# Local layers with four tiles in flight: shares divided on GpSimd, averages feature-major, projection of two tiles at once

## The chip, the cores and the metric

The kernel runs on one NeuronCore of a Trainium2 chip. The core has five engines that run side by side, each in its own order: TensorE (PE in the profile, with its weight loads shown as PEld), VectorE (DVE), ScalarE (ACT), GpSimd (POOL) and SyncE (SP), which here only issues transfers. Engines wait for each other through semaphores. Matmuls read SBUF and write PSUM[...]; GpSimd does not read PSUM in this kernel. The metric is the device time of one execution in microseconds.

## The reference, cut to what matters

The whole program is a stack of four layers (cross attention, routed feed-forward, windowed attention and so on). The change touches only the third layer's second half, a local transformer of six blocks (DEPTH = 6) over x of shape (4, 512, 128), with 16 heads of 64 features and windows of 32 tokens:

```python
def local_attention(q, k, v):          # q, k normalised and rotated
    bq = q.reshape(b, h, nw, w, d)     # w = 32
    bk2, bv2 = look(bk), look(bv)      # this window and the one before it: 64 keys
    sim = einsum('bhwie,bhwje->bhwij', bq, bk2) * 8.0
    sim = where(mask, -max, sim)       # only the 32 keys before a query and itself
    attn = softmax(sim, -1)
    out = einsum('bhwij,bhwje->bhwie', attn, bv2)
...
for i in range(DEPTH):
    x = attn_layer(shift_tokens(x), Wqkv[i], q_scale[i], k_scale[i], Wo[i]) + x
    x = ffn_layer(shift_tokens(x), ...) + x
```

`attn_layer` projects x to q, k and v (1024 features each), divides q and k by their length in each head, applies a rotation by position, attends as above and projects the 1024 features back to 128 with Wo. All values are fp32.

## The kernel before

The function `local_transformer` works on 96 tiles of 128 tokens: six blocks, four rows of the batch, four tiles a row (`tt` is 0 to 3). The residual stream Y is kept feature-major: 128 feature partitions by 512 tokens for each row. The loop at the end of the function runs over n, and one turn of it, here called a period, works on several tiles at once: T (tile n) is projected to q, k and v and rotated, T1 (tile n - 1) has its q and k transposed and its scores and softmax computed, T2 (tile n - 2) has its probabilities transposed, its averages taken and projected. Beside them F, a whole row of 512 tokens, goes through one of the four phases of the feed-forward: phase 0 takes the moments and normalises, phase 1 transposes and does the gate products of two chunks, phase 2 the gate of the third chunk and two up products, phase 3 the last up product and the down product. The order of the statements is written by hand (`manual_schedule`), and each engine executes its own instructions in exactly that order.

What a tile goes through, with the lines of the profile:

- `queries_or_keys` (L1780, L1782): a matmul of 512 columns, four a tile (two for q, two for k), and its square on ScalarE.
- `rotate` (L1790, L1793, L1802, L1803): two products and a sum over squares on VectorE, then an addition on GpSimd.
- `normalise` (L1813 to L1822): the inverse lengths, small operations on GpSimd and ScalarE, and four products on GpSimd.
- `turned` (L583 with rc, L1830 or L1832, L1834): q, then k, transposed on TensorE and copied by ScalarE. For k, GpSimd first copies the last 32 keys of the tile before (L1830), or zeros (L1832), to the front of kT.
- `scores` (L1878, L1887): mask and scores, 64 rows by 32 columns of the array at a time, into the two banks "sc".
- `softmax` (L1897, L1898, L1903): largest value and subtraction on VectorE, exponential on ScalarE. The sum is not taken here: v has a 65th column of ones (L1851), so that the averages carry their own sum.
- `probabilities` (L583 with P, L1908): P transposed and copied.
- `average` (L1918): four pairs of heads at a time, stationary P^T (64 keys by 32 queries), moving v (64 keys by 65), output token-major in the two banks "av".
- `normalised` (L1927, L1928): reciprocal of the 65th column and product, on VectorE, to attn.
- `attended` (L583 with attn, L1937): attn transposed to feature-major aT.
- `project_out` and `residual` (L1942, L1949): eight accumulating matmuls over 128 tokens, and the addition to Y in two halves of 64 partitions.
- `values` (L1857, L1858, and the DMAs from L1860 on): v for both halves of the heads, copied to v1, and shifted by a window into v2 by transfers on SP's queue.

The PSUM pair "sc" is shared by the scores and by the feed-forward's products, and the pair "av" by averages and projection. A new use of a pair waits for the last reader of the old one. Two banks "tr" serve all transposes and the values in turn, two banks "mm" the q and k products. P, PT, attn and aT have one buffer each, v1 and v2 three, the rotated tiles six.

## Time and profile before

| | |
|---|---|
| median of the runs | 2501.84 us (2493.18 to 2504.8, 3 runs) |
| profiled execution | 2497.58 us |
| its span, first to last instruction | 2495.8 us |
| granted TensorE clock, mean | 0.951 |
| busy PE / DVE / ACT / POOL | 90% / 70% / 52% / 55% |
| L1780 matmuls, first to last | 533.7 to 2150.7 us |

The span holds everything from the first instruction to the last. In a group's row the first numbers are the total busy time and the mean time of one instruction, and after the bar stands the idle time of its engine just before it and what ended that idle time. [...] how fast matmuls follow each other is read from the timeline, by the difference between the starts of neighbouring rows. An fp32 matmul stands in the trace as two records. A timeline row gives the start, the duration from the first start to the last end, the engine, the line, what is written and read, and how many instructions it merges; in brackets is the idle time before it with its releaser.

### The profile page before, as it was taken

To read this page: it belongs to the slowest core of one execution; us is meant where nothing else is said; L and a number is where in the kernel's file an instruction comes from. 1 tells how busy PE (TensorE), PEld (TensorE's weight loads), DVE (VectorE), ACT (ScalarE), POOL (GpSimd) and SP (SyncE) were. 2 spreads that over 40 slices of the span, in tenths; PEclk is the share of its full clock that TensorE was granted. 3 is DMA by queue.
4 is the path that set the end of the run, shared out by engine and by line. 5 is a ranking of instruction groups with operands and counts; after the bars stand their busy time and mean duration, and the time that the engine had idled before them with its cause. 6 is when DMAs were issued, how large, how long until landed. Compare 5 with 4: busy or idle time off the path is not lost.

```text
span 2495.8 us, 86737 instructions
## 1 busy us (share of the span) xinstructions
PE 2257.5 (90%) x37341; PEld 1487.1 (60%) x37341; DVE 1746.9 (70%) x3818; ACT 1292.4 (52%) x2379; POOL 1383.5 (55%) x1948
## 2 busy tenths in 40 slices
PE   7959879968999999999999999999999999978676
PEld 3537644536666666666666666666666666634365
DVE  5526355757788787778888888788788888655522
ACT  3513225545666556666666666556556666524232
POOL 2241232347667666676667766766667666432433
PEclk9959889989999999999999999999999999979788
DMA  6210110014411121111211121111211111111022
GB/s 162 84 39 23 37 42 2 1 49 95 120 34 35 30 57 50 27 35 35 69 35 35 30 76 35 30 31 39 65 35 35 33 29 35 29 39 47 21 74 83
DMA packets 134297, 116.14 MB, mean 47 GB/s; under 512 B 29505, under 2 KB 102700, under 8 KB 133916
## 3 DMA queue, kind: packets, MB, share of 16 engines
q1 hardware_dynamic: 128373, 102.81, 15.8%
q0 software_dynamic: 4608, 7.35, 0.9%
q8 instruction: 296, 4.85, 0.8%
q14 instruction: 85, 0.70, 0.1%
q10 hardware_dynamic: 935, 0.43, 0.1%
HBM read 42.84 MB, written 21.52 MB: 26 GB/s over the span
## 4 chain that ended last, share of the span: by engine, by line
PE 72%; DVE 15%; issue 4%; ACT 3%; DMA 2%; POOL 2%; another core or an unknown queue 2%; SPq 1%; POOLq 0%; ACTq 0%; DVEq 0%
PE ps_tr L583 12%; PE ps_mm L1780 10%; PE ps_av L1942 6%; PE ps_av L1918 5%; PE ps_tr L1857 5%; PE ps_sc L1887 4%; DVE xn L523 3%; PE ps_sc L1977 3%; PE ps_sc L1988 3%; PE ps_sc L2000 2%; PE ps L774 2%; PE ps L1313 2%; PE ps L783 2%; PE ps L1682 2%
## 5 line engine op out<-in xcount | busy, mean ns | idle before, releaser
L1803 POOL TENSOR_TENSOR rc<-rc,rs 128x512 f32<-128x512 f32 x384 | 489.5, 1276 | 385.4 <-DVE rs L1793 329.5
L1780 PE MATMUL ps_mm<-wqk,y 128*128 128x512 f32 x768 | 396.9, 599 | 10.5 <-DVE rs L1793 7.3
L1822 POOL TENSOR_TENSOR rc<-rc,rn_y 128x512 f32<-128x512 f32 x384 | 388.7, 1044 | 7.5
L1790 DVE TENSOR_TENSOR rc<-ps_mm,tabs 128x512 f32<-128x512 f32 x384 | 262.5, 684 | 137.8 <-ACT sq L1782 123.4
L1782 ACT ACTIVATE sq<-ps_mm 128x512 f32<-128x512 f32 x384 | 231.4, 603 | 166.9 <-PE ps_mm L1780 119.3
L1793 DVE TENSOR_TENSOR rs<-ps_mm,tabs 128x512 f32<-128x512 f32 x384 | 261.5, 681 | 1.6 <-POOL rc L1803 1.4
L1802 DVE TENSOR_REDUCE ss<-sq 128x8 f32<-128x512 f32 x384 | 259.5, 676 | 0.0
L583 PE MATMUL ps_tr<-cst,rc 128*128 128x128 f32 x1536 | 210.7, 280 | 6.8 <-issue 4.1
L1918 PEld LDWEIGHTS ps_av<-v,PT 64*32 64x32 f32 x12288 | 138.1, 105 | 124.5 <-PE ps_tr L583 55.8
L1942 PE MATMUL ps_av<-aT,wo 128*128 128x128 f32 x1536 | 199.6, 283 | 3.4 <-issue 3.2
L1942 PEld LDWEIGHTS ps_av<-aT,wo 128*128 128x128 f32 x1536 | 181.0, 193 | 12.7 <-issue 4.0
L583 PEld LDWEIGHTS ps_tr<-cst,rc 128*128 128x128 f32 x1536 | 164.6, 141 | 26.7 <-issue 4.7
L1918 PE MATMUL ps_av<-v,PT 64*32 64x65 f32 x12288 | 169.9, 225 | 4.6 <-DVE attn L1928 2.1
L1887 PE MATMUL ps_sc<-kT,qT 64*32 64x64 f32 x12288 | 146.8, 224 | 28.9 <-issue 26.8
L1018 POOL DMA_INDIRECT back<-ye,to x80 | 78.0, 975 | 162.0 <-DVE ye L1132 120.4
L1887 PEld LDWEIGHTS ps_sc<-kT,qT 64*32 64x32 f32 x12288 | 140.1, 105 | 39.1 <-issue 31.4
L1780 PEld LDWEIGHTS ps_mm<-wqk,y 128*128 128x128 f32 x768 | 124.6, 192 | 60.7 <-issue 48.8
L764 ACT ACTIVATE P<-ps,deltaT 77x512 f32<-77x512 f32 x192 | 115.4, 682 | 77.5 <-PE ps L758 69.9
L1903 ACT ACTIVATE P<-P 128x1024 f32<-128x1024 f32 x96 | 101.5, 1057 | 92.1 <-DVE P L1898 92.1
L1814 ACT ACTIVATE rn_y<-ss 128x32 f32<-128x32 f32 x96 | 22.0, 229 | 238.4 <-POOL ss L1813 238.4
L1834 ACT COPY qT<-ps_tr 128x512 f32<-128x512 f32 x192 | 103.3, 589 | 74.6 <-PE ps_tr L583 74.3
L1834 ACT COPY kT<-ps_tr 128x512 f32<-128x512 f32 x192 | 103.3, 589 | 66.2 <-PE ps_tr L583 65.9
(394 smaller groups left out, 4439.6 us busy)
## 6 DMA issues: line engine op xcount, KB each, us to landing
v<-v SPq DMA_DIRECT2D x432, 65.0 KB
v<-v SPq DMA_DIRECT2D x96, 195.0 KB
wqk<-in_L_ffn_Wqkv_dram SPq DMA_DIRECT2D x24, 256.0 KB
sent<-xn SPq DMA_DIRECT2D x2, 2210.0 KB
xe<-sent SPq DMA_DIRECT2D x16, 260.0 KB
back<-xn SPq DMA_DIRECT2D x2, 2048.0 KB
raw<-in_L_ffn_W_dram SPq DMA_DIRECT2D x8, 512.0 KB
yb<-back SPq DMA_DIRECT2D x16, 256.0 KB
```

The lines of the kernel that those rows point to most:

```text
L583: PE.transpose(t[:, i], src[:, i], ident)
L1780: PE.matmul(t, lhs, T.w[2 * kind + c], start=True, stop=True)
L1782: SC.activation(sq, t, AF.Square)
L1790: V.tensor_tensor(a, t, bc(T.tabs[:, 2 * kind, tt], [128, 8, LD], 1), ALU.mult)
L1793: V.tensor_tensor(r.rearrange("p h (x d) -> p h x d", x=2), t.rearrange("p h (x d) -> p h x d", x=2)[:, :, ::-1], bc(T.tabs[:, 2 * kind + ...
L1802: V.tensor_reduce(T.ss[:, kind, 8 * c : 8 * c + 8], sq, AX.X, ALU.add)
L1803: G.tensor_tensor(a, a, r, ALU.add)
L1822: G.tensor_tensor(a, a, bc(y[:, o : o + 8], [128, 8, LD], 2), ALU.mult)
L1834: SC.copy(t[:, 4 * c : 4 * c + 4, lead:], to_features(T.rot[kind, c].rearrange("p (k x) d -> p k (x d)", x=2)),)
L1887: PE.matmul(T.banks[32 * w : 32 * w + 32, z, k], T.qT[r, k, 32 * w : 32 * w + 32], T.kT[r, k, 32 * w : 32 * w + 64], start=False, stop=Tru ...
L1918: PE.matmul(T.means[32 * w : 32 * w + 32, x0, k], T.PT[r, 4 * g + k, 32 * w : 32 * w + 32], (T.v1 if w % 2 else T.v2)[r, x0, 4 * g + k], s ...
L1942: PE.matmul(t, T.wo[:, c], T.aT[:, c], start=(c == 0), stop=(c == 7))
```

## The change

The period now holds four tiles. T and T1 do what they did. T2 only sums its exponentials: the new `sums` takes the 16 sums and their reciprocals on VectorE, and the new `shares` multiplies P by them on GpSimd, in place, in two products of 128 by 512. T3 (tile n - 3) has its probabilities transposed, averaged and projected. P has two buffers, and v loses its column of ones.

`average` swaps the operands: v is stationary (64 keys by 64 features) and P^T moves (64 keys by 32 queries), so that the output is feature-major, 64 partitions at a time. The two calls, pairs of heads 0 to 3 and 4 to 7, fill the same pair of banks, with no reader between them. `normalised` is gone, and `attended` is two copies by ScalarE from PSUM into one half of an aT for 256 tokens; its eight transposes are gone. `project_out` and `residual` run for every second tile, over 256 columns.

In the order of statements: both halves of the average stand ahead of the first key product; `sums` and `shares` stand behind the second rotation; `attended` stands ahead of `turned(T1, 1)`, where before it stood behind the third rotation. The feed-forward phases, and the loading of the next block's weights, start one period later, and the loop has one more turn.

```diff
-                    T.v1 = vp.tile([128, 2, LH // 2, LD + 1], F32, name="v1")
-                    T.v2 = vp.tile([128, 2, LH // 2, LD + 1], F32, name="v2")
-                    G.memset(T.v1[:, :, :, LD : LD + 1], 1.0)
+                    T.v1 = vp.tile([128, 2, LH // 2, LD], F32, name="v1")
+                    T.v2 = vp.tile([128, 2, LH // 2, LD], F32, name="v2")
...
+            def sums(T):
+                T.sum = small.tile([128, LH // 2, 2], F32, name="la_sum")
+                V.tensor_reduce(T.sum, T.P, AX.X, ALU.add)
+                V.reciprocal(T.sum, T.sum)
+
+            def shares(T):
+                for g in range(2):
+                    k = slice(4 * g, 4 * g + 4)
+                    P = T.P[:, k].rearrange("p k z d -> p (k z) d")
+                    rec = T.sum[:, k].rearrange("p k z -> p (k z)")
+                    G.tensor_tensor(P, P, bc(rec, [128, 8, LD], 2), ALU.mult)
...
             def average(T, g):
                 if g == 0:
-                    T.attn = tp.tile([128, LH // 2, 2, LD], F32, name="attn", bufs=1)
-                T.means = pair("av")[:, :, : 4 * LD + 4].rearrange("p x (k d) -> p x k d", d=LD + 1)
-                for k in range(4):
+                    T.means = pair("av").rearrange("p s (k q) -> p s k q", q=64)
+                for k in range(4 * g, 4 * g + 4):
                     for w in range(4):
                         for x0 in range(2):
                             r = slice(64 * (x0 ^ (w // 2)), 64 * (x0 ^ (w // 2)) + 64)
+                            q = 32 * (w % 2)
                             PE.matmul(
-                                T.means[32 * w : 32 * w + 32, x0, k],
-                                T.PT[r, 4 * g + k, 32 * w : 32 * w + 32],
-                                (T.v1 if w % 2 else T.v2)[r, x0, 4 * g + k],
-                                start=True, stop=True,
+                                T.means[64 * x0 : 64 * x0 + 64, w // 2, k, q : q + 32],
+                                (T.v1 if w % 2 else T.v2)[r, x0, k],
+                                T.PT[r, k, 32 * w : 32 * w + 32], start=True, stop=True,
                             )
...
             def attended(T):
-                flat = T.attn.rearrange("p k x d -> p k (x d)")
-                T.aT = tp.tile([128, LH // 2, 128], F32, name="aT", bufs=1)
-                for g in range(2):
-                    SC.copy(T.aT[:, 4 * g : 4 * g + 4], to_features(flat[:, 4 * g : 4 * g + 4]))
+                if T.tt % 2 == 0:
+                    T.aT = tp.tile([128, LH // 2, 256], F32, name="aT", bufs=1)
+                else:
+                    T.aT = T.before.aT
+                for s in range(2):
+                    o = 128 * (T.tt % 2) + 64 * s
+                    SC.copy(T.aT[:, :, o : o + 64], T.means[:, s])
...
-                t = pair("av")[:, 0, :128]
+                t = pair("av")[:, 0, :256]
...
-                m, phase = divmod(n - 6, 4)
+                m, phase = divmod(n - 7, 4)
...
-                    if n % 16 == 7 and T.i + 1 < DEPTH:
+                    if n % 16 == 8 and T.i + 1 < DEPTH:
...
-                if T2:
-                    average(T2, 0)
+                if T3:
+                    average(T3, 0)
                 if T1:
                     turned(T1, 0)
+                if T3:
+                    average(T3, 1)
                 if T:
                     queries_or_keys(T, 1, 0)
-                if T2:
-                    normalised(T2, 0)
-                if T:
                     rotate(T, 0, 1)
                 if T2:
-                    average(T2, 1)
+                    sums(T2)
+                    shares(T2)
+                if T3:
+                    attended(T3)
                 if T1:
                     turned(T1, 1)
                 if T:
                     queries_or_keys(T, 1, 1)
-                if T2:
-                    normalised(T2, 1)
-                if T:
                     rotate(T, 1, 0)
-                if T2:
-                    attended(T2)
...
-                if T2:
-                    project_out(T2)
-                    residual(T2)
+                if T3 and T3.tt % 2:
+                    project_out(T3)
+                    residual(T3)
```

More of the change, by code (lines that the diff above doesn't have):

```diff
@@ L1857, in values @@
                 PE.matmul(t, src[:, 128 * tt : 128 * tt + 128], T.wv[:, x0], start=True, stop=True)
-                SC.copy(T.v1[:, x0, :, 0:LD], t)
+                SC.copy(T.v1[:, x0], t)
                 if x0 == 0:
@@ L1893, in softmax @@
             def softmax(T):
-                P = tp.tile([128, LH // 2, 2, LD], F32, name="P", bufs=1)
+                T.P = tp.tile([128, LH // 2, 2, LD], F32, name="P", bufs=2)
+                P = T.P.rearrange("p k z d -> p z k d")
                 mx = small.tile([128, 2, LH // 2], F32, name="la_mx")
                 V.tensor_reduce(mx, T.banks, AX.X, ALU.max)
-                V.tensor_tensor(
-                    P.rearrange("p k z d -> p z k d"), T.banks,
-                    bc(mx, [128, 2, LH // 2, LD], 3), ALU.subtract,
-                )
-                T.P = P.rearrange("p k z d -> p k (z d)")
-                SC.activation(T.P, T.P, AF.Exp, scale=8.0)
+                V.tensor_tensor(P, T.banks, bc(mx, [128, 2, LH // 2, LD], 3), ALU.subtract)
+                SC.activation(T.P, T.P, AF.Exp, scale=8.0)
+            def sums(T):
[8 more added lines that the diff above has]
+                    G.tensor_tensor(P, P, bc(rec, [128, 8, LD], 2), ALU.mult)
             def probabilities(T):
                 T.PT = tp.tile([128, LH // 2, 128], F32, name="PT", bufs=1)
+                P = T.P.rearrange("p k z d -> p k (z d)")
                 for g in range(2):
-                    SC.copy(T.PT[:, 4 * g : 4 * g + 4], to_features(T.P[:, 4 * g : 4 * g + 4]))
+                    SC.copy(T.PT[:, 4 * g : 4 * g + 4], to_features(P[:, 4 * g : 4 * g + 4]))
             def average(T, g):
                 if g == 0:
-                    T.attn = tp.tile([128, LH // 2, 2, LD], F32, name="attn", bufs=1)
-                T.means = pair("av")[:, :, : 4 * LD + 4].rearrange("p x (k d) -> p x k d", d=LD + 1)
-                for k in range(4):
+                    T.means = pair("av").rearrange("p s (k q) -> p s k q", q=64)
+                for k in range(4 * g, 4 * g + 4):
                     for w in range(4):
@@ L1917, in average @@
                             r = slice(64 * (x0 ^ (w // 2)), 64 * (x0 ^ (w // 2)) + 64)
+                            q = 32 * (w % 2)
                             PE.matmul(
-                                T.means[32 * w : 32 * w + 32, x0, k],
-                                T.PT[r, 4 * g + k, 32 * w : 32 * w + 32],
-                                (T.v1 if w % 2 else T.v2)[r, x0, 4 * g + k],
-                                start=True, stop=True,
-                            )
-            def normalised(T, g):
-                den = small.tile([128, 2, 4], F32, name="la_den")
-                V.reciprocal(den, T.means[:, :, :, LD])
-                V.tensor_tensor(
-                    T.attn[:, 4 * g : 4 * g + 4].rearrange("p k x d -> p x k d"),
-                    T.means[:, :, :, 0:LD], bc(den, [128, 2, 4, LD], 3), ALU.mult,
-                )
-            def attended(T):
-                flat = T.attn.rearrange("p k x d -> p k (x d)")
-                T.aT = tp.tile([128, LH // 2, 128], F32, name="aT", bufs=1)
-                for g in range(2):
-                    SC.copy(T.aT[:, 4 * g : 4 * g + 4], to_features(flat[:, 4 * g : 4 * g + 4]))
+                                T.means[64 * x0 : 64 * x0 + 64, w // 2, k, q : q + 32],
+                                (T.v1 if w % 2 else T.v2)[r, x0, k],
+                                T.PT[r, k, 32 * w : 32 * w + 32], start=True, stop=True,
+                            )
+            def attended(T):
+                if T.tt % 2 == 0:
[5 more added lines that the diff above has]
+                    SC.copy(T.aT[:, :, o : o + 64], T.means[:, s])
             def project_out(T):
-                t = pair("av")[:, 0, :128]
+                t = pair("av")[:, 0, :256]
                 for c in range(8):
@@ L1945, in residual @@
             def residual(T):
-                t = T.out
-                for r, o in ((slice(0, 64), 0), (slice(64, 128), 1)):
-                    dst = Y[T.b][r, 128 * T.tt + o : 128 * T.tt + o + 128]
+                t, o0 = T.out, 128 * (T.tt - 1)
+                for r, o in ((slice(0, 64), o0), (slice(64, 128), o0 + 1)):
+                    dst = Y[T.b][r, o : o + 256]
                     V.tensor_tensor(dst, t[r], dst, ALU.add)
@@ L2033, in local_transformer @@
             SC.preload_act_table_set(EXP_LN)
-            for n in range(len(tiles) + 10):
-                T = tiles[n] if n < len(tiles) else None
-                T1 = tiles[n - 1] if 0 <= n - 1 < len(tiles) else None
-                T2 = tiles[n - 2] if 0 <= n - 2 < len(tiles) else None
-                m, phase = divmod(n - 6, 4)
+            for n in range(len(tiles) + 11):
+                T, T1, T2, T3 = (tiles[n - k] if 0 <= n - k < len(tiles) else None for k in range(4))
+                m, phase = divmod(n - 7, 4)
                 F = rows[m] if 0 <= m < len(rows) else None
                 if T:
-                    if n % 16 == 7 and T.i + 1 < DEPTH:
+                    if n % 16 == 8 and T.i + 1 < DEPTH:
                         loaded[T.i + 1] = load(T.i + 1)
@@ L2053, in local_transformer @@
                     queries_or_keys(T, 0, 0)
-                if T2:
-                    probabilities(T2)
+                if T3:
+                    probabilities(T3)
                 if T:
@@ L2060, in local_transformer @@
                     ff_stage(F, phase, False)
-                if T2:
-                    average(T2, 0)
+                if T3:
+                    average(T3, 0)
                 if T1:
                     turned(T1, 0)
+                if T3:
+                    average(T3, 1)
                 if T:
                     queries_or_keys(T, 1, 0)
-                if T2:
-                    normalised(T2, 0)
-                if T:
                     rotate(T, 0, 1)
                 if T2:
-                    average(T2, 1)
+                    sums(T2)
+                    shares(T2)
+                if T3:
+                    attended(T3)
                 if T1:
@@ L2088, in local_transformer @@
                     rotate(T, 1, 1)
-                if T:
                     normalise(T)
@@ L2092, in local_transformer @@
                     softmax(T1)
-                if T2:
-                    project_out(T2)
-                    residual(T2)
+                if T3 and T3.tt % 2:
+                    project_out(T3)
+                    residual(T3)
                 if F and phase == 0:
```

## The prediction

> **What bounds the kernel now.** The table of busy shares comes first, then the chain that ended last, then the costliest groups, then the timeline of single periods, because shares average over stages with different limits.

> ```profile
> PE 2257.5 (90%) x37341; PEld 1487.1 (60%) x37341; DVE 1746.9 (70%) x3818; ACT 1292.4 (52%) x2379; POOL 1383.5 (55%) x1948
> ...
> PE 72%; DVE 15%; issue 4%; ACT 3%; DMA 2%; POOL 2%; another core or an unknown queue 2%; SPq 1%; POOLq 0%; ACTq 0%; DVEq 0%
> ...
> L1803 POOL TENSOR_TENSOR rc<-rc,rs 128x512 f32<-128x512 f32 x384 | 489.5, 1276 | 385.4 <-DVE rs L1793 329.5
> L1822 POOL TENSOR_TENSOR rc<-rc,rn_y 128x512 f32<-128x512 f32 x384 | 388.7, 1044 | 7.5
> L1918 PE MATMUL ps_av<-v,PT 64*32 64x65 f32 x12288 | 169.9, 225 | 4.6 <-DVE attn L1928 2.1
> ```

> TensorE is busy 90% and carries 72% of the chain, so removing its work looks like the way to gain. The changed stage, the local layers, runs from the first L1780 matmul (533.7 us) to the last (2150.7): 1617 us for 96 tiles, 16.84 us each. Its loop has four kinds of period, by the feed-forward phase in each. The windows view of four neighbours (columns: length, busy PE, PEld, DVE, ACT, POOL):

> ```profile
> 1211.30:1228.50 17.20, 16.87 (x331) 11.25 (x330) 11.79 (x20) 12.57 (x22) 11.41 (x17) 1.00 0.32 93
> 1228.50:1246.07 17.57, 17.57 (x333) 11.55 (x332) 14.00 (x23) 8.94 (x17) 12.26 (x18) 1.00 0.09 25
> 1246.07:1260.85 14.78, 14.63 (x330) 10.63 (x329) 14.15 (x30) 7.69 (x16) 9.14 (x14) 1.00 0.16 40
> 1260.85:1277.97 17.12, 16.78 (x333) 11.31 (x332) 15.32 (x25) 11.95 (x23) 12.60 (x19) 1.00 0.13 34
> ```

> They are phases 2, 3, 0, 1, together 66.67 us. In phase 0 VectorE is busy 14.15 of 14.78 us and the critical chain there leaves TensorE for it. So TensorE is the bound, but VectorE, ScalarE and GpSimd, each in order, are close behind in single places. The timelines of TensorE, ScalarE and GpSimd in phase 2 show the place I hold decisive, the start of the scores:

> ```profile
> 1219.25 1.02 PE L1780 MATMUL ps_mm<-wqk,y 128*128 128x512 f32 x2
> 1220.11 1.04 PE L583 MATMUL ps_tr<-cst,attn 128*128 128x128 f32 x8
> 1221.07 0.41 PE L1878 MATMUL ps_sc<-maskw,identb 64*32 64x512 bf16 x8
> 1221.30 1.46 PE L1887 MATMUL ps_sc<-kT,qT 64*32 64x64 f32 x128
> ...
> 1219.01 1.07 ACT L1834 COPY kT<-ps_tr 128x512 f32<-128x512 f32 x2 [0.31 <-PE ps_tr L583]
> 1220.36 0.60 ACT L1782 ACTIVATE sq<-ps_mm 128x512 f32<-128x512 f32 x1 [0.27 <-ACT kT L1834]
> 1220.85 1.07 ACT L1937 COPY aT<-ps_tr 128x512 f32<-128x512 f32 x2
> ...
> 1218.14 1.27 POOL L1803 TENSOR_TENSOR rc<-rc,rs 128x512 f32<-128x512 f32 x1 [1.61 <-DVE rs L1793]
> 1219.36 0.40 POOL L1830 COPY kT<-kT 128x256 f32<-128x256 f32 x1
> 1220.77 1.28 POOL L1803 TENSOR_TENSOR rc<-rc,rs 128x512 f32<-128x512 f32 x1 [1.02 <-PE ps_tr L583]
> ```

> Scores (L1887) need kT from two engines: the two copies on ScalarE (done 1220.08) and the 32-key lead on GpSimd (done 1219.76). Both have over 1.2 us to spare, because TensorE still does a key matmul and the transposes of attn after the transposes of k.

> **The change, part by part** (TensorE costs from start to next start).

> Transposes of attn removed: eight, pitch 0.11, -0.87 us a tile. ScalarE keeps two 0.59 us copies, now from the averages.

> Projection of two tiles: now 16 records in 1.89 us per tile (1272.65 to 1274.54). N=512 records follow each other at 0.43 us, so N=256 ones at 0.216: 3.46 us for two tiles, -0.16 a tile. But every second period has 3.46 and the other none: it falls into phases 1 and 3, already the longer ones.

> Averages: 64 records a half in both versions. Now eight 64x32 array tiles run side by side, 0.64 us plus 0.15 until the next matmul: 0.79. Then four 64x64 ones, 64 weight columns and 32 moving. No row shows 64x64. Low end: the present 0.79. High end: pairs of tiles taken one after the other, 0.107 us a pair of loads, 16 per half, plus 0.15: 1.9. Weight loads last 105 ns at 32 columns and 192 at 128, 0.9 ns a column; [...] I take 1.1 (loads 0.93 plus the gap), nearer the load row: +0.62 a tile for two halves. [...]

> TensorE in sum: -0.87 - 0.16 + 0.62 = -0.41 us a tile.

> VectorE: two reciprocals and two products out (0.8 a half, 1.65), one sum over 1024 elements (as L1897, 1.22) and a reciprocal (0.2) in; residual halves in number. It is near equal, but the sum stands between the second and third rotation.

> GpSimd: two products in, of L1822's form (1.044 each): +2.09 us, minus the 0.13 us memset of ones. [...] The row gives 1.044 against 0.692 for L1928, 1.5 times[...]. I use the row. Busy goes to 13.4 of 16.7 us, no bound by total. Behind these products in its queue stands the kT lead copy, and behind that scores wait.

> ScalarE: the two attended copies move from behind the fourth square to ahead of the kT copies, 1.1 us; the kT copies, the fourth square, the fourth rotation and the softmax are behind them.

> At nothing: v DMAs (2048 for 2080 bytes a row, one period more until use); the weight loads of the next layer, one period later on SP, seven periods (117 us) ahead of their use; with that cover gone, one wait a layer. Pipeline one tile deeper: one more thin period in the drain, +4 us once.

> **The four periods worked out.** Times are from the first query matmul. Phase 3: queries 0.86, transposes of P 0.87, queries 0.86, feed-forward 0.95, average 1.1, turned 0.93, average 1.1, keys at 6.65, turned at 7.5, keys, TensorE ready for scores at 9.3. ScalarE: third square 7.7 to 8.3 (it starts 1.1 after its matmul, as at 1252.03), attended to 9.3, first kT copy to 9.85, second to 10.4, fourth square to 10.95. VectorE: rotations (1.8 each) to 6.2, sum and reciprocal to 7.6. GpSimd: products 7.65 to 9.75, lead copy to 10.15. Scores start at 10.2; now 9.99 (1238.49). So 0.9 us of TensorE saving becomes a wait. Then 1.4 scores, 3.46 projection, 1.72 values, 2.58 feed-forward: 19.4.

> Phase 0: VectorE first has 1.5 us of residual, then the layer-norm moments (1.15) between rotations: sum done at 8.3, products to 10.4, lead 10.85, scores 10.9 (now 9.78). Fourth square 10.65, rotation to 12.5, softmax subtraction to 14.9, exponential 16.0, first v copy 16.6. No projection: TensorE is done at 14.0 but the next transposes of P need the bank of that v copy, so they start at 16.6 (now 16.08).

> Phase 1 from there: normalisation on VectorE to 1.8, rotations to 5.4, sum to 6.85, products to 9.0, lead 9.4, scores 9.45 (now 9.11); then 1.4 + 3.46 + 1.72 + 1.72: 17.75 (now 15.82).

> Phase 2: lead 9.9, scores 9.95 (now 10.0), values to 13.1; the up projection needs the score banks, which the softmax frees at 10.95 + 1.8 + 2.4 = 15.15 (now 14.1); no projection covers this; plus 1.72: 16.9.

> Sum 16.6 + 17.75 + 16.9 + 19.4 = 70.65 against 66.67: +1.0 us a tile, +96 us. With averages at 0.85 instead of 1.1 phases 0 and 2 shorten by half a us each, +70. I take +88, and +4 for the drain: 2497.58 (the profiled execution; its span 2495.8) becomes 2590. The median of the runs, 2501.84, is 4 above that execution: 2594, given as 2592.

> **Rivals.**

> Averages slow: [...] at 1.9 the keys come 1.6 us later each period and TensorE is ready after the lead copy: some +1.5 us a tile in all, 2645. For it: half the array tiles, in pairs. Against: queued loads of other tiles now start 7 ns apart.

> Waits half absorbed: were the lead copy always in time, phases 1 and 3 would lose 1.05 and 0.65 less: +0.57 a tile, 2560; with quick averages as well +0.36, 2540.

> The other side: TensorE alone decides, -0.41 x 96 + 4 = -35: 2467; with averages at 0.79, -99. Place: the first score matmul. It decides if kT, lead included, is there when TensorE is ready (8.2 to 9.3 us) in every period and the softmax leaves the banks before TensorE returns to them. For it: TensorE's 90%; GpSimd has idle time. Against: the sum is queued behind two rotations, and its end at 7.6 plus 2.1 plus 0.4 is 10.1.

> **How the numbers follow.** Chances: waits as worked out 0.57 (own range 2555 to 2625), slow averages 0.16, half absorbed 0.15, TensorE alone 0.12. The range 2505 to 2675 leaves out the last case and the tail of the second. A time 0.5% from before is what a measurement of this kernel can tell from no change. Faster 0.10 and same 0.04 come from the last case and the edge of the third, slower 0.86.

> **What would show it.** Right: GpSimd products before the lead copy at 9.5 to 11 us into each period; TensorE idle before the first score matmul, released by GpSimd's kT copy; the up projection waiting for the softmax in every fourth period; even and odd periods differing by some 2.5 us. Wrong: TensorE busy over 97% between 700 and 2000 us, no wait at the scores, or averages at 0.8 or over 1.5 us a half.

## The result, and the profile after

The changed kernel takes 2606.61 us (median of 4 runs, 2599.62 to 2612.25) against 2498.09 for the kernel before on the same chip: a ratio of 1.0421, 95% interval 1.0396 to 1.0446. The forecast was 2592 in a range of 2505 to 2675. The profiled execution took 2599.62 us with a span of 2597.8, 102 more than before.

The page of the changed kernel, busy shares and chain:

```profile
PE 2258.4 (87%) x35805; PEld 1446.1 (56%) x35805; DVE 1680.5 (65%) x3530; ACT 1279.6 (49%) x2379; POOL 1568.4 (60%) x2044
...
PE 64%; DVE 16%; issue 6%; ACT 4%; POOL 4%; DMA 2%; SPq 1%; another core or an unknown queue 1%; POOLq 0%; ACTq 0%; DVEq 0%
```

TensorE has 1536 records fewer and is busy as long as before; its share of the chain fell from 72% to 64%, and "issue" (nothing visible to wait for) and GpSimd gained. The local stage, from the first L1780 matmul (529.9 us) to the last (2239.0), takes 1709.1 us, 17.80 a tile, against 1617.0 and 16.84: 92 of the 102 us. Four neighbouring periods, phases 1, 2, 3 and 0 (length, busy PE, PEld, DVE, ACT, POOL):

```profile
1307.13:1326.95 19.82, 18.18 (x326) 12.37 (x325) 13.86 (x23) 12.55 (x23) 16.42 (x23) 1.00 0.13 34
1326.95:1344.19 17.24, 15.12 (x308) 9.16 (x307) 11.17 (x16) 12.03 (x22) 12.47 (x18) 1.00 0.07 19
1344.19:1363.64 19.45, 19.20 (x326) 12.63 (x325) 14.17 (x21) 8.96 (x18) 15.07 (x19) 1.00 0.16 44
1363.64:1377.69 14.05, 12.75 (x306) 8.65 (x305) 12.97 (x26) 7.53 (x16) 12.68 (x17) 1.00 0.09 21
```

They sum to 70.56 us. The long periods are the ones with a projection (326 records), and the short ones no longer keep TensorE busy: 12.75 of 14.05. The timelines of VectorE, GpSimd and TensorE in the last of these periods show the place that the prediction held decisive:

```profile
1370.37 1.21 DVE L1902 TENSOR_REDUCE la_sum<-P 128x16 f32<-128x1024 f32 x1
1371.62 0.25 DVE L1903 RECIPROCAL la_sum<-la_sum 128x16 f32<-128x16 f32 x1
...
1372.01 2.04 POOL L1911 TENSOR_TENSOR P<-P,la_sum 128x512 f32<-128x512 f32 x2 [0.64 <-DVE la_sum L1903]
1374.00 0.39 POOL L1830 COPY kT<-kT 128x256 f32<-128x256 f32 x1
...
1371.79 1.02 PE L1780 MATMUL ps_mm<-wqk,y 128*128 128x512 f32 x2
1372.74 0.41 PE L1876 MATMUL ps_sc<-maskw,identb 64*32 64x512 bf16 x8
1374.45 1.49 PE L1885 MATMUL ps_sc<-kT,qT 64*32 64x64 f32 x128 [1.30 <-POOL kT L1830]
```

Sum, reciprocal, two products, lead copy, and only then the scores: TensorE stood idle 1.30 us. In phase 3 the same wait is 0.25 us; in phases 1 and 2 the scores wait 0.21 us for ScalarE's kT copy instead. Two more waits of the same four periods, in phase 1 (transposes of P for the bank of the v copies) and in phase 2 (up projection for the softmax):

```profile
1309.58 1.14 PE L583 MATMUL ps_tr<-cst,P 128*128 128x128 f32 x8 [1.43 <-ACT v L1856]
1342.39 1.96 PE L1995 MATMUL ps_sc<-xnT,lw 128*128 128x512 f32 x4 [1.91 <-DVE P L1897]
```

The table of TensorE's waits over the whole run (us in total, times, longest):

```profile
PE ps_sc L1885 <- POOL kT L1830: 42.0, 52, 3.1
PE ps_tr L583 <- ACT v L1856: 36.9, 25, 2.4
PE ps_sc L1885 <- issue: 30.8, 16, 2.8
PE ps_sc L1995 <- DVE P L1897: 27.7, 19, 1.9
```

The first, second and fourth were forecast: they are the three waits just shown. In the kernel before, the only wait of this stage near that size was "scores, issue", 26.8 us. The third line, idle time without a releaser, was in neither the forecast nor any of its rivals.

### The profile page after: what moved, and what is told of

It is laid out like the page before. It is cut to its first block, busy times and chain, and to the rows that moved or that the text cites. A ratio compares the mean times of both kernels' runs of the same rounds, so it can differ in the third digit from the quotient of the medians.

```text
span 2597.8 us, 83333 instructions
## 1 busy us (share of the span) xinstructions
PE 2258.4 (87%) x35805; PEld 1446.1 (56%) x35805; DVE 1680.5 (65%) x3530; ACT 1279.6 (49%) x2379; POOL 1568.4 (60%) x2044
## 4 chain that ended last, share of the span: by engine, by line
PE 64%; DVE 16%; issue 6%; ACT 4%; POOL 4%; DMA 2%; SPq 1%; another core or an unknown queue 1%; POOLq 0%; ACTq 0%; DVEq 0%
PE ps_mm L1780 10%; PE ps_tr L583 8%; PE ps_av L1949 7%; PE ps_av L1929 5%; PE ps_sc L1885 4%; PE ps_tr L1855 4%; PE ps_sc L1995 3%; PE ps_sc L1984 3%; PE ps_sc L2007 2%; POOL P L1911 2%; DVE P L1897 2%; DVE la_mx L1896 2%; PE ps L774 2%; DVE rc L1790 2%; ACT kT L1834 2%
## 5 line engine op out<-in xcount | busy, mean ns | idle before, releaser
L1803 POOL TENSOR_TENSOR rc<-rc,rs 128x512 f32<-128x512 f32 x384 | 487.8, 1273 | 238.8 <-DVE rs L1793 170.3
L1780 PE MATMUL ps_mm<-wqk,y 128*128 128x512 f32 x768 | 408.4, 615 | 11.0 <-DVE rs L1793 7.7
L1822 POOL TENSOR_TENSOR rc<-rc,rn_y 128x512 f32<-128x512 f32 x384 | 388.2, 1042 | 7.5
L1782 ACT ACTIVATE sq<-ps_mm 128x512 f32<-128x512 f32 x384 | 236.2, 616 | 259.1 <-issue 137.9
L1793 DVE TENSOR_TENSOR rs<-ps_mm,tabs 128x512 f32<-128x512 f32 x384 | 261.1, 680 | 1.5 <-POOL rc L1803 1.4
L1911 POOL TENSOR_TENSOR P<-P,la_sum 128x512 f32<-128x512 f32 x192 | 196.1, 1042 | 74.3 <-DVE la_sum L1903 59.4
L1929 PEld LDWEIGHTS ps_av<-PT,v 64*64 64x64 f32 x12288 | 201.6, 134 | 64.3 <-issue 24.3
L1929 PE MATMUL ps_av<-PT,v 64*64 64x32 f32 x12288 | 222.7, 221 | 0.6 <-issue 0.5
L583 PE MATMUL ps_tr<-cst,rc 128*128 128x128 f32 x1536 | 205.1, 276 | 3.9 <-POOL rc L1822 3.9
L583 PEld LDWEIGHTS ps_tr<-cst,rc 128*128 128x128 f32 x1536 | 172.3, 141 | 60.3 <-issue 39.8
L1885 PEld LDWEIGHTS ps_sc<-kT,qT 64*32 64x32 f32 x12288 | 129.9, 105 | 114.4 <-POOL kT L1830 66.2
L1949 PE MATMUL ps_av<-aT,wo 128*128 128x256 f32 x768 | 183.1, 392 | 2.2 <-ACT aT L1943 1.2
L1780 PEld LDWEIGHTS ps_mm<-wqk,y 128*128 128x128 f32 x768 | 125.3, 193 | 67.7 <-issue 46.4
L1949 PEld LDWEIGHTS ps_av<-aT,wo 128*128 128x128 f32 x768 | 144.8, 194 | 25.8 <-issue 1.8
L1834 ACT COPY qT<-ps_tr 128x512 f32<-128x512 f32 x192 | 103.3, 589 | 92.8 <-PE ps_tr L583 92.4
L1898 ACT ACTIVATE P<-P 128x1024 f32<-128x1024 f32 x96 | 101.5, 1057 | 90.5 <-DVE P L1897 90.5
```

The source lines that it names most:

```text
L583: PE.transpose(t[:, i], src[:, i], ident)
L1780: PE.matmul(t, lhs, T.w[2 * kind + c], start=True, stop=True)
L1782: SC.activation(sq, t, AF.Square)
L1793: V.tensor_tensor(r.rearrange("p h (x d) -> p h x d", x=2), t.rearrange("p h (x d) -> p h x d", x=2)[:, :, ::-1], bc(T.tabs[:, 2 * kind + ...
L1803: G.tensor_tensor(a, a, r, ALU.add)
L1822: G.tensor_tensor(a, a, bc(y[:, o : o + 8], [128, 8, LD], 2), ALU.mult)
```

## The experiments

They ran on several chips, on which the kernel before took between 2453 and 2513 us. Each is given by its ratio to the kernel before on its own chip, to be held against 1.042. Times in the stage are from the traces.

### One part undone at a time

First, GpSimd's lead copy goes ahead of the sums and shares (the tile kT is allocated there):

```diff
+                if T1:
+                    leading(T1)      # kT = qp.tile(...); lead copy or memset on GpSimd
                 if T2:
                     sums(T2)
                     shares(T2)
```

> The changed kernel with GpSimd's copy of the 32 leading keys issued ahead of the sum and the shares. The wait list shows TensorE held at the first score matmul by that copy, 1.30 us in phase 0 and 0.25 in phase 3, so the simple theory (the copy's place is the cost) expects 1.55 us less in four tiles, 37 us less: 2570. My theory says the end of phase 0 is set by the v copies behind the softmax, and the softmax by the fourth square on ScalarE, which do not move: the wait only changes its place, 0.2 us in four tiles, 5 us less: 2595 to 2607.

Measured 2679.64 us, ratio 1.0911 (1.0856 to 1.0965): much slower, where both theories had it about level or faster. The waits of its TensorE, and the place where they hurt:

```profile
PE ps_tr L583 <- ACT v L1859: 70.4, 27, 3.6
PE ps_av L1952 <- issue: 52.5, 36, 3.8
PE ps_sc L1998 <- DVE P L1900: 42.0, 22, 1.9
```

```profile
1320.18 1.02 PE L1780 MATMUL ps_mm<-wqk,y 128*128 128x512 f32 x2
1323.81 1.94 PE L583 MATMUL ps_tr<-cst,P 128*128 128x128 f32 x8 [2.62 <-ACT v L1859]
1325.55 1.83 PE L1780 MATMUL ps_mm<-wqk,y 128*128 128x512 f32 x2
```

The wait for the lead copy is gone. TensorE reaches the transposes of P earlier and waits there longer, the work after such a wait often runs at half pace (1.94 us for eight transposes that take 1.03 elsewhere; the granted clock of this stretch, 0.50, is shown at the end), and 52 us without a releaser turned up inside the projection's own matmuls. The stage is 133 us longer than the changed kernel's. Of these, 67 us are more idle time, and some 61 are the clock: an estimate, the length of the stage times the share of the clock that was not granted (1842.6 us at a mean of 0.953, against 1709.1 at 0.985).

Second, the two attended copies on ScalarE go behind the fourth square:

```diff
-                if T3:
-                    attended(T3)
                 if T1:
                     turned(T1, 1)
                 if T:
                     queries_or_keys(T, 1, 1)
                     rotate(T, 1, 0)
+                if T3:
+                    attended(T3)
```

> The changed kernel with the two attended copies moved on ScalarE from ahead of the k copies to behind the fourth square. My theory: the fourth rotation and the softmax come 0.5 us earlier, which phase 2 (up products waiting for the softmax) gains in full; phase 1 gains 0.3 at the scores; phases 0 and 3 stay with the leading keys on GpSimd. 0.8 us in four tiles, 19 us less: 2588. A theory that only GpSimd's queue counts expects no change, 2607.

Measured 2507.56 us, ratio 1.0241 (1.0209 to 1.0272): 1.8% better than the changed kernel, over twice the forecast gain, and not where it was forecast. The up projection's wait for the softmax, which was to shrink, went from 27.7 to 30.3 us. In the stage, 39 us shorter, idle time fell by 21: the scores' wait for ScalarE's kT copies went (8.7 us), their wait for the lead copy fell by 4, and their idle time without a releaser by 11. How much the copies' place gained by itself, and how much came with a shift of that last kind of stall (explained below), this run does not divide. The prediction had this edit only as 1.1 us a tile ahead of the kT copies.

Third, both together.

> Both moves together, leading keys first and attended late. If the two queues cover for each other, the sum is more than the parts: 0.35 in phase 1, 0.5 in phase 2, 0.4 in phase 3, 0.5 in phase 0, 1.85 us in four tiles, 44 us less: 2563, against 24 less for the parts one by one. The simple theory of the leading keys expects what they give alone, 37 less.

Measured 2574.84 us, ratio 1.0498 (1.0475 to 1.0522): worse than the second alone and than the changed kernel, which both theories expected it to beat. With the lead copy first, time is lost here too.

Fourth, the projection of each tile by itself:

```diff
-                ...
+                T.aT = tp.tile([128, LH // 2, 128], F32, name="aT", bufs=1)
-                if T3 and T3.tt % 2:
+                if T3:
                     project_out(T3)
                     residual(T3)
```

> The changed kernel with the projection and the residual of each tile by itself, 128 columns in every period, as before the change; all else as changed. TensorE does more work, 0.1 us a tile, so a theory of TensorE's work alone expects 2607 to 2620. My theory: the pair falls into the long periods 1 and 3, which lose 1.66 us each (3.55 to 1.89), while in phases 2 and 0 the projection fills waits of 1.9 and 1.4 us that TensorE has anyway, +0.5 at most. 2.9 us less in four tiles, 69 us less: 2538.

Measured 2561.94 us, ratio 1.0463 (1.042 to 1.0506): no gain, where 69 us were forecast. The waits for v and for the softmax did vanish, as forecast. Instead scores waited 57.2 us for the lead copy and 53.3 us without a releaser, and the projection's records took 195.6 us in the stage in place of 165.8.

At this point one of the four edits had gained, one had gained nothing, and two had lost, though each of these three had removed a wait that the trace names.

### Control, and two single suspects

> The changed kernel itself, beside the next three on one chip, since the first four experiments were compared with it only through its ratio to the kernel before on another chip. If that ratio carries over: 1.042, within 0.004. If it does not (1.03 or less, or 1.055 or more), the four earlier verdicts have to be read again against the value found here.

Measured 2604.19 us, ratio 1.0412 (1.0366 to 1.0458): the changed kernel's ratio is the same on two chips, on which the kernel before took 2498 and 2500 us. On the chip of the first four experiments (2453 us) the changed kernel itself was not run, so their ratios can be set beside 1.042 only roughly, which matters for the third and fourth. The stage of the fifth's trace is 1724.8 us where the result's has 1709.1, with the same idle time (156.2) and more half clock: 15 us between two traces say little by themselves.

The sixth adds to the first that the softmax's exponential moves behind the two v copies on ScalarE:

```diff
                     values(T, 0)
                     values(T, 1)
+                if T1:
+                    exponential(T1)   # taken out of softmax
```

> The lead copy ahead of the sums and shares, as in the first experiment (ratio 1.091), and besides the softmax's exponential moved behind the two v copies on ScalarE. Theory one: what the first experiment lost is the wait of the transposes of P for the v copies (27 waits, 70 us together) and the matmuls that ran at half speed after it (some 36 more slow key matmuls, 0.9 us each): with the v copies early both go, about -105 us, ratio 1.05 or a little under. Theory two, instruction supply: the wait for v only shows a stall which the instruction fetches would have made anyway, and it turns up again as an idle time without a releaser in the projection or the scores: ratio 1.08 to 1.09.

Measured 2681.61 us, ratio 1.0721 (1.0674 to 1.0768). Between the two theories: the wait of the transposes of P fell from 70.4 us (for the v copies) to 25.4 (now for GpSimd's step of the normalisation, L1817), so some of the first experiment's loss was that; the stall in the projection stayed (50.1 us).

The seventh adds the same to the second.

> The attended copies behind the fourth square, as in the second experiment (ratio 1.024), and the softmax's exponential behind the v copies. Theory one, waits add up: the 36 us of waits of the transposes of P for v go: ratio 1.010. Theory two, instruction supply: where that wait is taken away the fetches stall in its place: ratio 1.024 or above, with more idle time without a releaser (18 us before). If the exponential's delay (1.2 us) reaches the sums of the next period: 1.03 or above, with waits for the sums on GpSimd.

Measured 2561.35 us, ratio 1.0237 (1.0191 to 1.0283), no different from the second, and not for the reason that either theory gave. The waits for v are gone, and "issue" did not grow. Scores now wait longer for the lead copy:

```profile
PE ps_sc L1885 <- POOL kT L1830: 61.5, 71, 2.9
PE ps_sc L1997 <- DVE P L1897: 18.8, 21, 1.0
PE ps_sc L1885 <- issue: 18.0, 14, 4.4
```

The lead wait was 39.0 us in the second. A TensorE that comes early at one place of a period comes early at the next and waits there.

The eighth puts the shares on VectorE instead of GpSimd (one letter: `V.tensor_tensor` for `G.tensor_tensor` in `shares`).

> The changed kernel with the two products of the shares on VectorE instead of GpSimd. Simple theory, GpSimd behind VectorE's sum is what delays the lead copy: products take 0.7 instead of 1.04 each and the lead copy waits for none of them, about -0.4 us a tile, ratio 1.027. Mine: the same products now stand ahead of the third rotation on VectorE, which works already 11 to 14 of 14 to 19 us a period; the kT copies, the softmax and the release of the score banks come 1.4 us later, the lead copy only 2 us earlier than it needs: ratio 1.045 to 1.05, with longer waits of the feed-forward for the softmax.

Measured 2640.19 us, ratio 1.0552 (1.0496 to 1.0608): slower than with GpSimd, by more than either theory said. The lead wait vanished, but the wait for v doubled to 70.1 us. GpSimd, though it takes 1.042 us for a product that VectorE does in 0.69, is the better place here: the faster product took one wait away and brought another. Against the fifth experiment, on the same chip, the stage is 32 us longer. Only 9 of them are more idle time, since the two waits nearly balance; some 29 are the clock (estimated as above, mean 0.958 against 0.974), and single waits are longer (after the first rows 15 of 3.1 to 3.2 us, in the fifth one).

### The stall that no engine causes

In the sixth experiment's trace TensorE stops in the middle of the projection, whose operands are all there:

```profile
1302.57 1.66 PE L1888 MATMUL ps_sc<-kT,qT 64*32 64x64 f32 x128 [0.21 <-ACT kT L1837]
1304.16 1.13 PE L1954 MATMUL ps_av<-aT,wo 128*128 128x256 f32 x4
1306.26 2.75 PE L1954 MATMUL ps_av<-aT,wo 128*128 128x256 f32 x12 [0.97 <-issue]
```

The page of the changed kernel has a DMA queue of this kind (packets, MB):

```profile
q8 instruction: 283, 4.64, 0.7%
```

Where that boundary falls in a period follows from the number of instructions ahead of it. Two periods of the changed kernel have nearly 1280 instructions, 5 times 256, so the boundary stays almost at one place through the whole stage. It moves by 7 instructions in four periods in the changed kernel, by 1 in the first and sixth experiments. In what follows, the position is that of the boundary counted from the first score instruction of a tile; a score run is 256 instructions long and takes 1.4 us.

The ninth experiment tests this by adding work. It is the sixth with useless matmuls once before the stage:

```diff
+            t = pair("sc")[0:32, 0, 0:64]
+            for _ in range(108):
+                PE.matmul(t, identb[0:64, 0:32], maskw[0:64, 0, 0], start=True, stop=True)
             for n in range(len(tiles) + 11):
```

> The kernel of the sixth experiment (lead copy first, exponential behind the v copies, ratio 1.072) with 108 useless bf16 matmuls of 64 columns put once before the local layers: 216 more TensorE instructions, some 6 us of work, nothing else changed. Theory, instruction supply: in every kernel so far TensorE's stalls without a releaser lie at one place of its instruction stream, instruction 193 or 194 of each 256, and they cost time where that place falls between the 175th and the 275th instruction counted from the start of a score run. In the sixth experiment it falls there in phases 1 and 3 all through the stage (72 us of stalls). 216 more instructions move it to about the 140th in phases 0 and 2 and the 45th in phases 1 and 3: the stalls go, and the useless work makes the kernel faster by 50 to 90 us, ratio 1.04 to 1.052. Rival, the stalls belong to the projection itself (its operand aT, its bank[...]): they stay where they are, ratio 1.073 to 1.076.

Measured 2595.92 us, ratio 1.0342 (1.0304 to 1.0379) against 1.0721: 108 useless matmuls, which took 5.7 us, made the kernel 3.5% faster, more than the 1.04 to 1.052 that was expected. A projection of the same kind as above, now in one piece and with all sixteen records:

```profile
1286.39 1.47 PE L1888 MATMUL ps_sc<-kT,qT 64*32 64x64 f32 x128 [0.21 <-ACT kT L1837]
1287.80 3.72 PE L1954 MATMUL ps_av<-aT,wo 128*128 128x256 f32 x16
```

In the stage the projection's records fell from 196.6 to 165.2 us and the idle time before them from 49.3 to 5.1, together 76 of the 84 us by which the stage became shorter. The rival, a stall that belongs to the projection, is out. A control with a whole block of useless matmuls (128), which adds work and leaves the place where it is, was not run; that the place counts, and not the added work, rests on the positions below.

The tenth takes all three named waits away at once (lead first, attended late, exponential behind v); the eleventh is the tenth with 91 useless matmuls.

> Lead copy first, attended copies behind the fourth square, exponential behind the v copies: all three waits of the changed kernel that the trace names before scores and transposes taken away at once. Simple theory of waits: against the third experiment (1.050) the waits for v go as well (64 us): ratio 1.025. With instruction supply: the third experiment had 58 us of stalls at the 256-instruction place in phases 1 and 3, these stay or grow: ratio 1.03 to 1.05, with over 50 us of idle time without a releaser.

> The same with 91 of the useless matmuls (182 instructions, 5 us) before the local layers, which by the positions in the third experiment moves the 256-instruction place to about the 150th in phases 0 and 2 and the 50th in phases 1 and 3. Instruction supply: 45 to 60 us faster than the run before it in spite of the added work, ratio 1.00 to 1.02, and fewer than 15 us of stalls within one line's matmuls. Rival, stalls bound to the projection or the scores: 5 us slower than the run before it.

Measured 2611.12 us, ratio 1.0402 (1.0355 to 1.045), and 2552.25 us, ratio 1.0164 (1.0126 to 1.0203). The tenth has every edit that should help and is as slow as the changed kernel. Its largest waits in this stage:

```profile
PE ps_sc L1888 <- issue: 67.3, 33, 6.0
PE ps_sc L2000 <- DVE P L1900: 38.0, 22, 1.7
```

The eleventh gains 59 us by useless work alone. One number of its expectation missed: stalls of 34 us remained around the scores, where under 15 were expected, since the position was estimated from the third experiment and came out up to 197 instead of about 150. Stalls at the boundary in and around the scores, by position (after the first row of tiles):

| run | phases 0 and 2: position, us | phases 1 and 3: position, us |
|---|---|---|
| sixth | 98 to 125, 0 | 248 to 270, 72 |
| ninth | 139 to 166, 9 | 33 to 55, 11 |
| tenth | 53 to 119, 0 | 205 to 268, 76 |
| eleventh | 127 to 197, 28 | 23 to 86, 6 |

Taken over the changed kernel and all twelve experiments, without the first rows, a gap of over 0.8 us stands at 252 of 454 boundaries between position 160 and 280, and at 3 of 1521 outside. Within, it depends on the place: 16 of 83 between 160 and 180, 93 of 97 between 240 and 260. In the stretch of the sixth experiment above, the packet starts (1303.98) while the last scores run (1302.57 to 1304.23), 256 instructions in 1.4 us. Why the block doesn't come earlier, no run here shows.

The twelfth puts the three findings together: lead first, attended late, exponential behind v; the up projection of phase 2 in the averages' banks; normalisation behind the v copies where no projection follows; and the boundary kept in place.

```diff
             def ff_up(F, *chunks):
-                t = pair("sc")
+                t = pair("sc" if chunks == (2,) else "av")
...
                     rotate(T, 1, 1)
-                    normalise(T)
+                    if T3 and T3.tt % 2:
+                        normalise(T)
...
                     values(T, 1)
+                    if not (T3 and T3.tt % 2):
+                        normalise(T)
...
                 T.banks = pair("sc").rearrange("p z (k d) -> p z k d", d=64)
+                for j in range({0: 105, 48: 106}.get(tiles.index(T), 0)):
+                    ...  # a bf16 matmul of 64 columns into T.banks, overwritten by the masks
```

> The eleventh experiment with the three largest waits left in it taken away. Its up projection of the feed-forward waits for the softmax to leave the score banks (23 us): here it goes to the banks of the averages, which are free in that period. In periods without a projection the normalisation's ScalarE steps come behind the v copies, so that the transposes of P find their bank free (21 us). And the place of the 256-instruction boundary, counted by the instruction stream from the start of each score run, is held between 124 and 172 in phases 0 and 2 and between 16 and 60 in phases 1 and 3 by 105 useless bf16 matmuls before the first scores and 106 more before the 49th tile's (some 3 us each), against 29 us of stalls with it up to 197 in the run before. If the three add up, 22 + 23 + 21 - 3 = 63 us off 2552: ratio 0.99. If TensorE meets the next engine instead (VectorE works 14 of 14.8 us in phase 0, 12 to 13 elsewhere), half of it is lost: ratio 1.00 to 1.005. Rival, the place of the boundary matters only by chance: 1.01 or above.

Measured 2439.62 us (6 runs) against 2460.95, ratio 0.9911 (0.9891 to 0.9931): the forecast 0.99, and 0.9% faster than the kernel before. TensorE's two largest waits in this stage:

```profile
PE ps_av L1941 <- issue: 21.3, 24, 5.2
PE ps_av L1941 <- ACT PT L1929: 18.3, 26, 1.3
```

None of the three named waits of the changed kernel is left, and the scores' idle time without a releaser is down to 10.0 us; what there is lies in the averages. How the 62 us against the eleventh divide over the three new edits wasn't tried, nor what the new places of the normalisation and of the boundary would give the kernel before.

## Why the prediction was right, point by point

TensorE in the local stage, from the traces (us; idle counts gaps over 0.1):

| | stage | idle | work | of the work, lost to the clock (estimate) |
|---|---|---|---|---|
| before | 1617.0 | 57.2 | 1559.8 | 10 |
| after | 1709.1 | 156.0 | 1553.0 | 25 |
| twelfth (another chip) | 1607.7 | 66.9 | 1540.8 | 18 |

The estimate is the stage times the share of the clock that was not granted. Work without it lies between 1508 and 1552 us in all 14 traces, whose stages last from 1608 to 1843: most of the difference between the kernels is idle time and what the clock takes.

What ended TensorE's idle time in the stage (us):

| released by | before | after |
|---|---|---|
| GpSimd's lead copy, before scores | 2.1 | 43.0 |
| ScalarE's kT copies, before scores | 0 | 8.7 |
| v copies, before transposes of P | 5.9 | 34.6 |
| softmax, before the up projection | 0 | 27.7 |
| nothing visible, before scores | 26.0 | 28.2 |
| the rest | 23.2 | 13.8 |

The first four rows grew by 106 us, more than the whole growth of the idle time (99). So the mechanism of the forecast is what the trace shows: work put ahead in the queues of GpSimd and ScalarE, and waits of TensorE behind it.

**The four periods** were forecast at 70.65 us and measure 70.56 in the row shown. One by one, in the forecast's way of counting (phase 0 up to the transposes of P behind it, 1293.09 to 1309.58), phases 3, 0, 1 and 2 measure 19.45, 16.49, 17.37 and 17.24, forecast 19.4, 16.6, 17.75 and 16.9. The mean over all rows is 71.2: other rows have boundary stalls (30 us in the stage) or stretches at half clock (mean granted clock of the stage 0.985), which that row doesn't have (1.00). Stage +92 against +88 forecast; the other 10 us of the span lie outside it, where the sum had 4.

**Single terms.** Averages 1.09 us a half, start to start (1366.76 to 1367.85 is one), against 1.1. That 1.1 was the author's estimate: the loads' 0.93 are sixteen of 64 columns at 0.906 ns a column, the slope between 105 ns at 32 columns and 192 at 128, and the gap is 0.15. A projection pair 3.55 us against 3.46. Shares 1042 ns against 1044, 1.5 times the 692 ns of VectorE's product (L1928 of the kernel before), as the forecast took it. The lead copy's end in phase 0 comes 10.75 us into the period (forecast 10.85), the scores 10.81 (10.9).

**The step that was mis-sized: "TensorE in sum: -0.41 us a tile".** By the table it measured -0.07 (-6.8 us over 96 tiles, not -39). The edited lines gave more than was forecast, in the stage: averages 153.3 to 203.1, transposes of attn 90.5 to 0, projection 178.3 to 165.8, sum -53. But matmuls that nobody edited took some 46 us more. 17 of these are the masks: they take 0.41 us for eight (1372.74 above), as against 0.23 from start to start before, where the scores start (1221.30) ahead of their end (1221.48); scores that wait (1374.45) start behind it. They are a wait that the table counts as work. Some 15 are the clock (the estimate of the table, 25 less 10), a term that the sum did not have. What the other 14 are stays open; the value matmuls (+15) and the key and query matmuls (+11), which took the most, have a part of the clock's 15 in them. With the masks and the clock the waits come to 131 us (99 + 17 + 15) where the sum had 127, so they were sized about right. That the 14 us which the edited lines gave beyond the forecast were lost again elsewhere is luck, and makes the total fit better than its parts.

**The step left too small: the attended copies.** "1.1 us" on ScalarE ahead of the kT copies stood in the sum only through later stages. Undoing it gave 1.8% (some 45 us, second experiment), close to half the loss, where 19 us were expected. Part of that gain was idle time without a releaser (11 us of the stage), so 45 is the most that this place costs.

**Missing: the instruction boundary.** Gaps at the boundary came to 30 us in the changed kernel's stage and to 32 in that of the kernel before, so they add nothing to the difference. That is luck of the position: the sixth and ninth experiments, whose programs differ in the useless matmuls alone, are 84 us of stage apart.

**The rivals.** "TensorE alone decides" gave 2467, 1.4% faster than before, on the condition that the lead is there in every period and the softmax leaves the banks in time. The twelfth experiment supplies these conditions and comes to 0.9% faster. What of this is owed to the removed matmuls is not shown, since the kernel before never had the boundary kept in place, and its boundary gaps (32 us) are larger than the gain. In the changed kernel, the 53 us that the edited lines gave stand against the 106 us of waits in the table. "Waits half absorbed" (2540 to 2560) is near the second experiment (1.0241, 2558 on the chip of the result), but only in number: it supposed the lead copy always in time, and in the second experiment the scores still wait 39.0 us for it. Slow averages are out by 1.09.

## What to carry to other kernels

When work moves to an idle engine, write down what stands behind it in that engine's queue and who waits for that, period by period; the sum of those waits decides, and a busy share of 60% says nothing on it. A wait taken from the bounding engine is a gain only if the next one in the period isn't already due: take them away together, and expect little of one alone (in the seventh experiment the waits for v went and the lead wait grew from 39.0 to 61.5 us). And before an order is judged by one run, look whether its stalls sit at a fixed count of instructions: then a few useless instructions elsewhere can change the time by more than the edit does (59 us between the tenth and eleventh). Look also at the granted clock after long waits, since such a wait can cost more than its length (in the first, 2.62 us were followed by 3.4 us at a clock of 0.50).

## What the runs showed of the hardware that was not expected

TensorE's stalls inside one line's work keep to one place in every 256 of its instructions (by the counts above one packet of 16 KB): 420 of 466 gaps, over 14 traces, lie at index 192 to 195. In the changed kernel's stage 13 of its 18 gaps there last 1.2 to 2.8 us, all 13 in the scores. 108 added matmuls gained 3.5%.

A wait of 2.62 us cost more than itself. In the first experiment the windows around the wait at 1323.81 show the granted clock (the third figure from the right):

```profile
1321.00:1323.80 2.80, 0.20 (x1) 0.02 (x1) 2.13 (x5) 2.10 (x5) 1.92 (x5) 0.99 0.00 0
1323.80:1327.20 3.40, 3.39 (x10) 2.32 (x11) 1.88 (x3) 2.03 (x4) 3.40 (x5) 0.50 0.43 116
```

For 3.4 us after it TensorE ran at half clock (0.50): eight transposes in 1.94 us in place of 1.03, two key matmuls in 1.83 in place of 1.02. The length of a wait alone does not decide: in the first experiment, after its first rows, 13 of the 24 waits of 2.6 us were followed by a mean granted clock under 0.9 in the next 2 us, in the ninth 13 of 18 waits of 1.9. After the waits of 1.30 and 1.43 us shown from the changed kernel the clock stayed at 1.00. The stage of the first experiment has 52 key matmul records of over 0.7 us, where the changed kernel has 16.

VectorE's application of the layer norm (L523) had a median of 1080 ns before and 341 after, with the same instruction and shape:

```profile
L523 DVE TENSOR_SCALAR xn<-xn,ln_mv,ln_rs x96: 341/1080/1180, 648.6 to 2193.2; 128x128 f32<-128x128 f32 x96
```

```profile
L523 DVE TENSOR_SCALAR xn<-xn,ln_mv,ln_rs x96: 335/341/1081, 661.9 to 2291.5; 128x128 f32<-128x128 f32 x96
```

The first line is of the kernel before, the second of the changed one (shortest, median and longest ns). In the kernel before, 76 of the 96 ran beside GpSimd's products (L1822), with a median of 1081 ns, and the other 20 took at most 348. In the changed one 16 ran beside them, with a median of 1078, and the other 80, most of them beside GpSimd's smaller steps L1818 and L1819, took at most 345. So it is the company of these products that goes with the long time. What in the chip ties the two, no run here shows.
